# Two graph attentions in a GNN kernel: q and the exponentials in PSUM, weighted rows in buffers of their own, and the second attention in source order

## The chip, the cores and the metric

One core of one Trainium2 chip runs the whole program. The metric is the device time of one execution in microseconds (us). Engines: PE (TensorE), DVE (VectorE), ACT (ScalarE), POOL (GpSimd) and SP (SyncE); the last issues DMAs only. All data are float32.

## The reference

Four layers, each a graph step and a feed-forward step, on 3125 nodes of 256 features and 103125 edges (both directions and a loop at each node). The change touches the two attentions (layers 1 and 2). Layer 2's, cut down:

```
Q = (h @ Wq).reshape(n, H, HD); K, V likewise          # H = 8 heads
score = einsum('ehd,ehd->eh', Q[dst], K[src]) / sqrt(HD)
score = score + relu(efeat @ W1 + b1) @ W2 + b2        # the edge scores
m = segment_max(score, dst); ex = exp(score - m[dst])
alpha = ex / segment_sum(ex, dst)[dst]
out = segment_sum(alpha[:, :, None] * V[src], dst) @ Wo + bo
```
Layer 1's is of the same kind with 4 heads, keys and values by edge type, and no edge scores.

## The kernel before

The nodes are sorted by their number of edges and cut into 25 tiles of 128 nodes, one node to a partition. Tile t has CAPS[t] slots for edges (67, 44, 42 ... 22; 859 in all). A tile of more than KMAX = 44 slots is cut into parts: the first into two, so there are 26 parts, counted here from 0. A part is worked in chunks of CH = 4 slots: 225 chunks in all.

`attend` (L2299) does both attentions. For a part: q, the tile's 128 query rows, is loaded by SP (L2313). For every slot of a chunk POOL issues one indirect DMA (L2321) that gathers 128 rows of 2 KB (key and value of each node's neighbour) from a table in HBM into `kv`, by a column of indices in SBUF. DVE multiplies the key halves by q in place (L2326) and reduces the products to scores `s` (L2330). After the last chunk DVE adds the mask or edge scores (L2337), takes the maximum (L2339, L2341) and subtracts it (L2342); ACT takes exponentials (L2345); DVE sums them to `den` (L2347), and multiplies the value halves of each chunk by them in place (L2351). PE adds the weighted rows up by products with the identity into `u` in PSUM (L2361), two slots to a matmul. ACT copies one half of u to `agg` (L2366), DVE adds the other (L2367) and divides by den (L2389). `post` turns agg by PE (`turned_tile`, L2394, its copy L2400), multiplies it by the output weights and adds it to x (L833 in the first attention, L2650 in the second).

Buffers: `kv` has 13 of 8 KB per partition, and one comes free when PE has read its weighted rows. PSUM has two `u`.

The first attention carries a generator, `scores` (`edge_scores`, L1930): before each chunk's q product `next(beside, None)` emits a step of the second layer's edge scores: matmuls into `ph` and `psc`, relus by ACT (L1972), a turn by PE into `pst` (L1989). So its PE has work of its own.

The order of each engine's instructions is set by the framework's scheduler from its estimates, not by the source, except inside a block under `tc.manual_schedule(engines=...)`, where the engines named follow the source.

Of the kernel before, what the change touches and what calls it, by code (L numbers as in the profile page):

```python
# [23 lines left out]
F = mybir.dt.float32  # L24
I32 = mybir.dt.int32
U32 = mybir.dt.uint32
AF = mybir.ActivationFunctionType
OP = mybir.AluOpType
# [5 lines left out]
P = 128  # L34
# [32 lines left out]
class Net:  # L67
# [1862 lines left out]
    def edge_scores(self, ctx):  # L1930

        nc, tc, a, heads = self.nc, self.tc, self.a, 8
        pool = ctx.enter_context(tc.tile_pool(name="sc", bufs=1))
        wp = ctx.enter_context(tc.tile_pool(name="sc_w", bufs=2))
        ps_h = ctx.enter_context(tc.tile_pool(name="sc_h", bufs=1, space=PSUM))
        ps_s = ctx.enter_context(tc.tile_pool(name="sc_s", bufs=1, space=PSUM))
        w1 = pool.tile([P, D], F, name="w1")
        for s in range(2):  # L1940
            nc.sync.dma_start(w1[s * 64 : (s + 1) * 64], a["L2_gnn_W1"])
        b1 = self.columns(pool, a["L2_gnn_b1"], "b1")
        w2 = pool.tile([P, 2, 32], F, name="w2")
        nc.vector.memset(w2, 0.0)
        nc.sync.dma_start(w2[:, :, :heads], a["L2_gnn_W2"].rearrange("(c p) m -> p c m", p=P))
        b2 = pool.tile([P, 1], F, name="b2")
        nc.vector.memset(b2, 0.0)
        for k in range(4):
            nc.sync.dma_start(b2[32 * k : 32 * k + heads], a["L2_gnn_b2"].unsqueeze(1))

        def steps():
            for e0 in range(0, EP, STEP):
                pairs = min(STEP, EP - e0) // 1024
                runs = 2 * pairs
                ef = wp.tile([P, 2, 512], F, name="ef")
                for k in range(runs):
                    s, i = k % 2, k // 2
                    nc.sync.dma_start(
                        ef[s * 64 : (s + 1) * 64, i, :],
                        a["edge_t"][:, e0 + k * 512 : e0 + (k + 1) * 512],  # L1960
                    )
                hs = []
                for i in range(pairs):
                    h = wp.tile([P, 2, 2, 512], F, name="eh")
                    for f in range(2):
                        ps = ps_h.tile([P, 2, 512], F, name="ph")
                        for s in range(2):
                            half = slice(s * 64, (s + 1) * 64)
                            self.mm(
                                ps[:, s, :], [(w1[half, f * P : (f + 1) * P], ef[half, i, :])]  # L1970
                            )
                        nc.scalar.activation(h[:, f], ps, AF.Relu, bias=b1[:, f, :])  # L1972
                    hs.append(h)
                    yield
                ps = ps_s.tile([P, 512], F, name="psc")
                rows = 32 * runs
                for f in range(2):
                    for k in range(runs):
                        nc.tensor.matmul(
                            ps[32 * k : 32 * (k + 1)], w2[:, f, :], hs[k // 2][:, f, k % 2, :],  # L1980
                            start=f == 0, stop=f == 1,
                        )
                sc = wp.tile([P, 512], F, name="sc")
                nc.scalar.activation(sc[:rows], ps[:rows], AF.Identity, bias=b2[:rows])
                yield

                ps = ps_s.tile([P, 4, P], F, name="pst")
                for c in range(4):
                    nc.tensor.transpose(  # L1989
                        ps[:, c, :rows], sc[:rows].rearrange("h (p c) -> h c p", c=4)[:, c, :],  # L1990
                        self.ident[:rows, :rows],
                    )
                by_edge = wp.tile([P, 4, 4, heads], F, name="by_edge")
                nc.scalar.copy(
                    by_edge[:, :runs].rearrange("p k c h -> p c k h"),
                    ps[:, :, :rows].rearrange("p c (k r) -> p c k r", r=32)[:, :, :, :heads],
                )
                nc.scalar.dma_start(
                    self.score_d[e0 : e0 + runs * 512].rearrange(
                        "(k p c) h -> p k (c h)", c=4, p=P  # L2000
                    ),
                    by_edge[:, :runs].rearrange("p k c h -> p k (c h)"),
                )
                yield

        return steps()
# [292 lines left out]
    def attend(self, heads, q_d, table, rows, extra, post, beside=iter(())):  # L2299
# [3 lines left out]
        nc, tc = self.nc, self.tc  # L2303
        hd = D // heads
        with ExitStack() as sub:
            kvp = sub.enter_context(tc.tile_pool(name="at_kv", bufs=13))
            wp = sub.enter_context(tc.tile_pool(name="at_w", bufs=2))
            psu = sub.enter_context(tc.tile_pool(name="at_u", bufs=2, space=PSUM))
            held = None
            for t, k0, k, first, final in self.parts():  # L2310
                if first:
                    q = wp.tile([P, D], F, name="q")
                    nc.sync.dma_start(q, q_d[t * P : (t + 1) * P])  # L2313
                s = wp.tile([P, heads, KMAX], F, name="s")
                chunks = []
                for c0 in range(0, k, CH):
                    n = min(CH, k - c0)
                    kv = kvp.tile([P, CH, 2 * D], F, name="kv")
                    for c in range(n):
                        at = OFFS[t] + k0 + c0 + c  # L2320
                        nc.gpsimd.indirect_dma_start(  # L2321
                            out=kv[:, c, :], out_offset=None, in_=table,
                            in_offset=bass.IndirectOffsetOnAxis(ap=rows[:, at : at + 1], axis=0),
                        )
                    next(beside, None)
                    nc.vector.tensor_tensor(  # L2326
                        kv[:, :n, :D], kv[:, :n, :D], q.unsqueeze(1).to_broadcast([P, n, D]),
                        op=OP.mult,
                    )
                    nc.vector.tensor_reduce(  # L2330
                        s[:, :, c0 : c0 + n].rearrange("p h c -> p c h"),
                        kv[:, :n, :D].rearrange("p c (h d) -> p c h d", h=heads),
                        axis=AX.X, op=OP.add,
                    )
                    chunks.append((c0, n, kv))
# [6 lines left out]
                nc.vector.tensor_tensor(  # L2342
                    sk, sk, most.unsqueeze(2).to_broadcast([P, heads, k]), op=OP.subtract
                )
                nc.scalar.activation(sk, sk, AF.Exp)  # L2345
                den = wp.tile([P, heads], F, name="den")
                nc.vector.tensor_reduce(den, sk, axis=AX.X, op=OP.add)  # L2347
                u = psu.tile([P, 2, D], F, name="u")
                for c0, n, kv in chunks:
                    v = kv[:, :n, D:].rearrange("p c (h d) -> p c h d", h=heads)  # L2350
                    nc.vector.tensor_tensor(  # L2351
                        v, v,
                        s[:, :, c0 : c0 + n].rearrange("p h c -> p c h").unsqueeze(3).to_broadcast(
                            [P, n, heads, hd]
                        ),
                        op=OP.mult,
                    )
                    if n % 2:
                        nc.vector.memset(kv[:, n, D:], 0.0)
                    for c in range(0, n, 2):  # L2360
                        nc.tensor.matmul(  # L2361
                            u, self.ident, kv[:, c : c + 2, D:],
                            start=c0 == 0 and c == 0, stop=c0 + c + 2 >= k,
                        )
                agg = wp.tile([P, D], F, name="agg")
# [25 lines left out]
                )  # L2391
                post(t, agg)

    def turned_tile(self, psum, wp, rows):  # L2394

        ps = psum.tile([P, 2, P], F, name="tt")
        for c in range(2):
            self.nc.tensor.transpose(ps[:, c, :], rows[:, c * P : (c + 1) * P], self.ident)  # L2398
        sb = wp.tile([P, 2, P], F, name="tt_sb")
        self.nc.scalar.copy(sb, ps)  # L2400
        return sb
# [183 lines left out]
    def gnn2_ordered(self):  # L2585
        nc, tc, a = self.nc, self.tc, self.a
        heads, hd = 8, 32
        with ExitStack() as ctx:
# [44 lines left out]
            with ExitStack() as sub:  # L2633
# [9 lines left out]

                def post(t, agg):
                    at = self.turned_tile(psum, wp, agg)
                    po = psum.tile([P, D], F, name="o")
                    self.mm(
                        po, [(self.ones, bo)] + [(at[:, c, :], wo[:, c, :]) for c in range(2)]
                    )
                    nc.vector.tensor_tensor(self.x[:, t, :], self.x[:, t, :], po, op=OP.add)  # L2650

                self.attend(heads, q_d, kv_tab, self.row_src, extra, post)

    def gnn3_ordered(self):

# [257 lines left out]
```

## Time and profile before

| | us |
|---|---|
| median of 3 runs | 7778.85 (7748.85 to 7783.94) |
| the profiled execution | 7774.44 |
| its span | 7772.7 |
| first attention, first gather to the last update of x | 2346 to 3776 |
| second attention, the same | 4467 to 5804 |

Over the span PE is busy 4789.8 us (62%), POOL 3566.9 (46%), DVE 3206.6 (41%), ACT 1289.0 (17%); the mean granted clock of PE is 0.787. These shares average stages with different limits; the two attentions are read by their own stretches. In a row of grouped instructions the figures behind the bar are the busy time in us, the mean ns of one, and the engine's idle time just before them with what ended it. In a timeline row they are the start and length in us, the engine, line and operation, the tiles written and read, and in brackets the idle time before it.

### The profile page before, as it was taken

The page shows a single profiled execution, that of the slowest core. Times are in us where ns is not written, and L with a number is a line of the kernel's source. Part 1 is how long each engine was busy: PE and PEld are TensorE (multiplying, and loading weights), DVE is VectorE, ACT ScalarE, POOL GpSimd, SP SyncE. Part 2 cuts the span into 40 slices and gives each one's busy share as a digit, 9 for nine tenths or more (in the row PEclk, how much of TensorE's full clock was granted, in tenths as well). Part 3 has the DMA queues.
Part 4 walks back from the last instruction along what each step waited for, and adds up shares of the span by engine and source line. Part 5 has one row for each costly group of instructions (what it writes and reads, how often), then busy time and mean ns, then how long its engine had stood idle before and what let it go on. Part 6 is the DMA issues. An engine that isn't in the chain of part 4 may idle for free. (4 is left out here: it accounts for less than half of the span.)

```text
span 7772.7 us, 53026 instructions
## 1 busy us (share of the span) xinstructions
PE 4789.8 (62%) x17097; PEld 2917.2 (38%) x17097; DVE 3206.6 (41%) x5563; ACT 1289.0 (17%) x1898; POOL 3566.9 (46%) x4051
## 2 busy tenths in 40 slices
PE   1463313379885778878539423434452995498998
PEld 0352212244441222222338211111122995387554
DVE  7461101034224566666601255666672002496111
ACT  0000000022111222222013100000000221264222
POOL 3878787710006677776322377777752112100001
PEclk9786656689896888988669766666665997698999
DMA  6203542350336566666225255556641443221000
GB/s 246 86 18 123 178 178 69 92 163 9 139 138 185 166 188 199 198 186 175 86 99 181 90 166 170 171 172 178 183 137 72 168 170 107 102 73 38 9 13 22
DMA packets 424876, 999.32 MB, mean 129 GB/s; under 512 B 115151, under 2 KB 219057, under 8 KB 412942
## 3 DMA queue, kind: packets, MB, share of 16 engines
q0 software_dynamic: 206208, 656.36, 27.6%
q1 hardware_dynamic: 164616, 260.15, 10.3%
q10 hardware_dynamic: 53766, 79.32, 2.8%
q8 instruction: 141, 2.31, 0.1%
q14 instruction: 145, 1.19, 0.1%
HBM read 764.22 MB, written 231.45 MB: 128 GB/s over the span
## 5 line engine op out<-in xcount | busy, mean ns | idle before, releaser
L2321 POOL DMA_INDIRECT kv<-o_kv,row_et x859 | 974.9, 1135 | 432.9 <-issue 227.7
L2361 PE MATMUL u<-kv,ident 128*128 128x512 f32 x1740 | 880.9, 652 | 443.9 <-issue 332.7
L2321 POOL DMA_INDIRECT kv<-o_kv,row_src x859 | 1001.3, 1166 | 310.2 <-issue 229.3
L2145 POOL DMA_INDIRECT dense<-pair,place x859 | 907.5, 1056 | 294.5 <-issue 172.7
L2326 DVE TENSOR_TENSOR kv<-kv,q 128x1024 f32<-128x1024 f32 (+2 forms) x450 | 528.5, 1177 | 1022.1 <-DMA kv<-o_kv,row_src 561.6
L258 PE MATMUL g_u<-h_own,dense_rows 128*128 128x256 f32 x1250 | 389.2, 477 | 749.7 <-issue 234.9
L2361 PEld LDWEIGHTS u<-kv,ident 128*128 128x128 f32 x1740 | 340.7, 207 | 967.1 <-issue 792.0
L258 PEld LDWEIGHTS g_u<-h_own,dense_rows 128*128 128x128 f32 x1250 | 297.5, 246 | 841.1 <-issue 445.4
L2330 DVE TENSOR_REDUCE s<-kv 128x16 f32<-128x1024 f32 (+4 forms) x450 | 518.3, 1165 | 4.2
L2020 POOL DMA_INDIRECT out_dram<-x,order_i x25 | 24.6, 983 | 1051.5 <-DVE x L833 1006.6
L2351 DVE TENSOR_TENSOR kv<-kv,s 128x1024 f32<-128x1024 f32 (+2 forms) x450 | 496.5, 1169 | 0.0
L258 PE MATMUL c_hp<-c_xt,c_w 128*128 128x256 f32 x1536 | 389.6, 410 | 1.3 <-DVE c_xt L1251 1.3
L2028 POOL DMA_INDIRECT o_kv<-kv_rows,order_i x50 | 48.8, 976 | 716.9 <-ACT kv_rows L2524 483.9
L258 PE MATMUL ph<-ef,w 64*128 64x512 f32 x808 | 322.8, 709 | 88.6 <-issue 50.8
L258 PEld LDWEIGHTS c_hp<-c_xt,c_w 128*128 128x128 f32 x1536 | 371.7, 333 | 14.9 <-DVE c_xt L1251 7.5
L258 PE MATMUL c_o<-c_w,c_h 128*128 128x256 f32 x1536 | 351.9, 379 | 0.0
L2271 DVE TENSOR_TENSOR o_acc<-o_acc,g_u 128x256 f32<-128x256 f32 x125 | 52.3, 420 | 692.2 <-PE g_u L258 314.5
L1972 ACT ACTIVATE eh<-ph,b 128x1024 f32<-128x1024 f32 x202 | 224.9, 1114 | 499.5 <-PE ph L258 340.3
L2763 PE MATMUL u<-hs_all,eT_sb 128*128 128x256 f32 x1250 | 293.7, 382 | 21.9 <-ACT eT_sb L2759 21.9
L258 PEld LDWEIGHTS c_o<-c_w,c_h 128*128 128x128 f32 x1536 | 288.8, 191 | 34.9
L2398 PE MATMUL tt<-ident,agg 128*128 128x128 f32 x100 | 31.3, 412 | 420.8 <-DVE agg L2389 318.6
L833 DVE SCALAR_TENSOR_TENSOR x<-o,router_l,x 128x256 f32<-128x256 f32 x200 | 94.3, 484 | 459.2 <-PE o L258 459.2
(428 smaller groups left out, 7403.9 us busy)
## 6 DMA issues: line engine op xcount, KB each, us to landing
dense_rows<-dense SPq DMA_DIRECT2D x125, 640.0 KB
dense<-zero ACTq DMA_DIRECT2D x20, 3200.0 KB
ef<-in_edge_t_dram SPq DMA_DIRECT2D x202, 128.0 KB
number_d<-number SPq DMA_DIRECT2D x125, 160.0 KB
number<-number_d SPq DMA_DIRECT2D x25, 800.0 KB
c_x<-slot_d SPq DMA_DIRECT2D x64, 256.0 KB
result_d<-c_y SPq DMA_DIRECT2D x64, 256.0 KB
dense<-zero SPq DMA_DIRECT2D x5, 3200.0 KB
```

The source lines that it names most:

```text
L258: self.nc.tensor.matmul(ps, lhsT, rhs, start=i == 0, stop=i == len(pairs) - 1)
L833: self.nc.vector.scalar_tensor_tensor(self.x[:, t, :], y, w, self.x[:, t, :], op0=OP.mult, op1=OP.add)
L1972: nc.scalar.activation(h[:, f], ps, AF.Relu, bias=b1[:, f, :])
L2028: self.nc.gpsimd.indirect_dma_start(out=table, out_offset=bass.IndirectOffsetOnAxis(ap=self.order_i[:, t : t + 1], axis=0), in_=rows, in_o ...
L2145: nc.gpsimd.indirect_dma_start(out=dense[t], out_offset=bass.IndirectOffsetOnAxis(ap=place[:, at : at + 1], axis=0), in_=pair[:, at, :], i ...
L2271: nc.vector.tensor_tensor(acc[:, b, :], acc[:, b, :], ps, op=OP.add)
L2321: nc.gpsimd.indirect_dma_start(out=kv[:, c, :], out_offset=None, in_=table, in_offset=bass.IndirectOffsetOnAxis(ap=rows[:, at : at + 1], a ...
L2326: nc.vector.tensor_tensor(kv[:, :n, :D], kv[:, :n, :D], q.unsqueeze(1).to_broadcast([P, n, D]), op=OP.mult,)
L2330: nc.vector.tensor_reduce(s[:, :, c0 : c0 + n].rearrange("p h c -> p c h"), kv[:, :n, :D].rearrange("p c (h d) -> p c h d", h=heads), axis ...
L2351: nc.vector.tensor_tensor(v, v, s[:, :, c0 : c0 + n].rearrange("p h c -> p c h").unsqueeze(3).to_broadcast([P, n, heads, hd]), op=OP.mult,)
L2361: nc.tensor.matmul(u, self.ident, kv[:, c : c + 2, D:], start=c0 == 0 and c == 0, stop=c0 + c + 2 >= k,)
L2763: nc.tensor.matmul(u, et[:, j * P : (j + 1) * P], hs_all[:, b, :D], start=b == 0, stop=b == NT - 1,)
```

## The change

In both attentions, q is copied by ACT from its SBUF tile into a PSUM tile `q_ps`, from which DVE's product reads it; the exponentials are written to a PSUM tile `e`, from which den and the weighting products read; and the weighted value rows go into buffers of their own, `wv`, which PE's sums read. The first attention has 11 kv, 6 wv and one u; the second 12, 7 and two. To fit in PSUM, `psc` and `pst` share one buffer, and so do `turned_tile` and the output product `o`.

The second attention moves to a new function, `attend_in_order`, whose POOL, DVE, PE and ACT follow the source. There the weighting of a part is cut into steps: behind the scoring of each chunk of the next part come two chunks of it (three in parts of over 36 slots). Its sums by PE are emitted one chunk later (`sum_up`), and what follows them (`finish`, with `post`) is a list of steps, one to a chunk (`step_behind`), with empty steps between. q of the next tile is loaded at the second chunk of a tile's last part.

```
-            kvp = sub.enter_context(tc.tile_pool(name="at_kv", bufs=13))
+            kvp = sub.enter_context(tc.tile_pool(name="at_kv", bufs=11))
+            vp = sub.enter_context(tc.tile_pool(name="at_v", bufs=6))
-            psu = sub.enter_context(tc.tile_pool(name="at_u", bufs=2, space=PSUM))
+            psu = sub.enter_context(tc.tile_pool(name="at_u", bufs=1, space=PSUM))
...
                     nc.sync.dma_start(q, q_d[t * P : (t + 1) * P])
+                    q_ps = psu.tile([P, D], F, name="q_ps", bufs=2)
+                    nc.scalar.copy(q_ps, q)
...
-                        kv[:, :n, :D], kv[:, :n, :D], q.unsqueeze(1).to_broadcast([P, n, D]),
+                        kv[:, :n, :D], kv[:, :n, :D],
+                        q_ps.unsqueeze(1).to_broadcast([P, n, D]), op=OP.mult,
...
-                nc.scalar.activation(sk, sk, AF.Exp)
+                e = psu.tile([P, 512], F, name="e")[:, : heads * k]
+                e = e.rearrange("p (h c) -> p h c", h=heads)
+                nc.scalar.activation(e, sk, AF.Exp)
-                nc.vector.tensor_reduce(den, sk, axis=AX.X, op=OP.add)
+                nc.vector.tensor_reduce(den, e, axis=AX.X, op=OP.add)
...
+                    wv = vp.tile([P, CH, D], F, name="wv")
                     nc.vector.tensor_tensor(
-                        v, v,
-                        s[:, :, c0 : c0 + n].rearrange("p h c -> p c h").unsqueeze(3).to_broadcast(
+                        wv[:, :n, :].rearrange("p c (h d) -> p c h d", h=heads), v,
+                        e[:, :, c0 : c0 + n].rearrange("p h c -> p c h").unsqueeze(3).to_broadcast(
...
-                            u, self.ident, kv[:, c : c + 2, D:],
+                            u, self.ident, wv[:, c : c + 2, :],
```
The new function, without what is as in `attend`:

```
+    def attend_in_order(self, heads, q_d, table, rows, extra, post):
...
+            kvp = sub.enter_context(tc.tile_pool(name="at_kv", bufs=12))
+            vp = sub.enter_context(tc.tile_pool(name="at_v", bufs=7))
...
+                tc.manual_schedule(engines={E.Pool, E.DVE, E.PE, E.Activation})
...
+            def finish(part, u, most, den):
...
+                yield
+                agg = wp.tile([P, D], F, name="agg", bufs=3)
+                nc.scalar.copy(agg, u[:, 0, :])
+                yield
+                yield
+                nc.vector.tensor_tensor(agg, agg, u[:, 1, :], op=OP.add)
...
+                yield
+                yield from post(t, agg)
...
+            def weighed(part, chunks, e, most):
...
+                while len(unread) > 1:
+                    sum_up()
+                    step_behind()
+                unread.append(part)
+                den = wp.tile([P, heads], F, name="den", bufs=3)
+                nc.vector.tensor_reduce(den, e, axis=AX.X, op=OP.add)
+                u = psu.tile([P, 2, D], F, name="u", bufs=2)
+                for c0, n, kv in chunks:
...
+                    sums.append(lambda c=(c0, n, wv): add_up([c], u, k))
+                    yield
+                behind.append(finish(part, u, most, den))
...
+            for part in self.parts():
...
+                pace = 2 if k <= 9 * CH else 3
+                for c0 in range(0, k, CH):
...
+                    step_behind()
+                    sum_up()
+                    if c0 == CH and final:
+                        load_q(t + 1)
...
+                    step_weigh(pace)
+                    chunks.append((c0, n, kv))
+                while weigh:
+                    step_weigh(1)
```
And in what both call, and in the second attention's `post`:

```
-                ps = ps_s.tile([P, 4, P], F, name="pst")
+                ps = ps_s.tile([P, 512], F, name="psc").rearrange("p (c n) -> p c n", c=4)
...
-        ps = psum.tile([P, 2, P], F, name="tt")
+        ps = psum.tile([P, 2, D], F, name="o").rearrange("p a d -> p (a d)")
+        ps = ps[:, :D].rearrange("p (c n) -> p c n", c=2)
...
                     at = self.turned_tile(psum, wp, agg)
-                    po = psum.tile([P, D], F, name="o")
+                    yield
+                    po = psum.tile([P, 2, D], F, name="o")[:, 0, :]
...
+                    yield
+                    yield
+                    yield
                     nc.vector.tensor_tensor(self.x[:, t, :], self.x[:, t, :], po, op=OP.add)
 
-                self.attend(heads, q_d, kv_tab, self.row_src, extra, post)
+                self.attend_in_order(heads, q_d, kv_tab, self.row_src, extra, post)
```

## The prediction

> **What bounds the kernel now.** I read first the page (one core, span 7772.7 us), then its costliest groups: the three dearest contain the two gathers of L2321, one set per attention. Next the table by stretches for the two attentions, the waits of POOL, and the timeline at one part boundary.
>
> ```profile
> L2321 POOL DMA_INDIRECT kv<-o_kv,row_et x859 | 974.9, 1135 | 432.9 <-issue 227.7 <-PE u L2361 145.4 <-DVE kv L2351 14.6
> L2321 POOL DMA_INDIRECT kv<-o_kv,row_src x859 | 1001.3, 1166 | 310.2 <-issue 229.3 <-PE u L2361 55.6 <-DMA kv<-o_kv,row_src 12.5
> ```
> ```profile
> core 0: us, PE busy (x) PEld busy (x) DVE busy (x) ACT busy (x) POOL busy (x), PEclk, DMA share, GB/s
> 2346.00:3780.00 1434.00, 1088.52 (x2940) 350.42 (x2940) 864.47 (x1076) 300.68 (x385) 976.96 (x862) 0.84 0.63 180
> 4467.00:5804.00 1337.00, 530.35 (x1066) 231.72 (x1066) 831.98 (x953) 30.36 (x79) 1001.28 (x859) 0.66 0.59 171
> 3100.00:3300.00 200.00, 170.61 (x500) 53.89 (x500) 133.32 (x162) 54.15 (x69) 143.42 (x129) 0.93 0.68 197
> 4949.00:4966.00 17.00, 0.92 (x1) 0.50 (x2) 10.84 (x15) 0.46 (x1) 11.71 (x13) 0.50 0.74 215
> ```
> The attentions take 1434 and 1337 us. POOL is busy 75% of the second and DVE 62%; in the first PE has 76%, and 85% in its densest 200 us. The last row is a stretch in which every gather starts 1.25 us after the one before: DMA carries 215 GB/s there with 26% to spare, and elsewhere less, so it isn't the limit. Now how one gather behaves:
>
> ```profile
> 4962.17 0.95 POOL L2321 DMA_INDIRECT kv<-o_kv,row_src  x1 [0.30 <-issue]
> 4963.42 0.95 POOL L2321 DMA_INDIRECT kv<-o_kv,row_src  x1 [0.30 <-issue]
> 4964.90 9.50 DVE L2351 TENSOR_TENSOR kv<-kv,s 128x1024 f32<-128x1024 f32 x9
> 4969.11 6.12 POOL L2321 DMA_INDIRECT kv<-o_kv,row_src  x1 [4.74 <-PE u L2361]
> 4975.54 0.95 POOL L2321 DMA_INDIRECT kv<-o_kv,row_src  x1 [0.30 <-issue]
> ```
> The reader sees three things. An undisturbed gather takes 0.95 us and the next starts 0.30 us later: a pitch of 1.25 us. A gather may wait for a kv buffer that PE has still to read (4.74 us). And one that starts under the chain of products of L2351 is held until the chain is over: 6.12 us.
>
> I sorted all 859 gathers of the second attention by what DVE ran 0.2 us into each, and added up their time over 0.945 us: 220 under the q product L2326 are 90.0 us over, 89 under L2351 94.5 us over; but 153 under the reduction L2330 only 0.4, 293 under an idle DVE 0.2. All together 190; in the first attention 163. The two stretching forms read two operands from SBUF, the reduction one. What of two operands with one in PSUM?
>
> ```profile
> L2367 DVE TENSOR_TENSOR agg<-agg,u 128x256 f32<-128x256 f32 x26 | 10.7, 410 | 11.0 <-ACT agg L2366 7.3 <-issue 3.8
> L2389 DVE TENSOR_TENSOR agg<-agg,den 128x256 f32<-128x256 f32 x25 | 10.5, 421 | 0.1
> ```
> Nineteen gathers started under L2367 (u is in PSUM): 0.003 us over in all; 14 under L2650: 0.02; 31 under L833 in the first attention: 0.005; 12 under L2389 (both in SBUF): 0.7. And L2367 takes 410 ns against 421. So PSUM costs DVE nothing and frees POOL.
>
> **A rule against it.** The Trainium skill, "SBUF — State Buffer", section "Who interferes with whom", says that a DVE instruction with two SBUF inputs contends with GpSimd instructions that read SBUF, not with those that only write, and it infers that descriptor generation needs only the write side, so that tensor_tensor had not stalled DMA in its probe. By that inference products would not delay gathers and this part of the sum would be 0 instead of 353. The rows above speak against the inference (these gathers do read their index column from SBUF); I take the trace.
>
> **The change, part by part: second attention (before: first gather 4467.1, last ends 5776.0, result 5803).**
> - Floor: 859 gathers x 1.25 = 1074 us, against 1309 now. Of the 235 between, 190 are stretching and 48 are waits beyond the 0.305 us gap (310.2 - 859 x 0.305).
> - q and e in PSUM: -190, save for L2337, L2342 and L2389, which keep two SBUF inputs (4 us of the 190): -186.
> - kv buffers come free after DVE's product instead of after PE's sum, but there are 12 in place of 13. With nine chunks to a part POOL can run 3 chunks (15 us) ahead. The first buffer is free 12 us after the part's end: last chunk lands (gather to DVE 3.8 us), product and reduction 2.4, the part's four small operations 2.5, the next first chunk's product and reduction 2.4, den and one product 1.6. So no wait; with ten chunks (4 parts) POOL is 10 us ahead and waits 2, with eleven (2 parts) 5 us ahead and waits 7. Sum 22 us in place of 48: -26.
> - Order by chunks: DVE does two or three of the old part's products behind each chunk, so the chain of 10 us goes. Per chunk: four operations of about 1.15 us of busy time, against 5.0 us of gathers. DVE's 832 us in 1137 is 73%: covered by POOL. If that cover failed, each DVE us counts.
> - Steps spaced over chunks: the agg copy, the sum, turned_tile, po and the x update each come a chunk (5 us) behind what they wait for, so DVE, PE and ACT, now in source order, do not stand in front of a late wait. If one step stood, the next chunk's product would queue behind it on DVE: 26 parts x about 1 us; I take 10 us.
> - q: SP issues the load (25 x 0.32 us; it has nothing else here) nearly a tile earlier, and ACT adds 25 copies of about 0.37 us (row L2400) beside its 30 us of work: hidden. POOL's order of gathers stays. An ACT write to PSUM has no row; nearest is the L2366 copy out of it, 372 ns.
> - wv: same number of products, memsets and matmuls. Tail after the last gather: 27 us now, the same after.
> Sum: -186 - 26 + 10 = -202; bounds -235 (floor) and -100 (DVE stands behind ordered waits half the time gained). I take -200.
>
> A second rule bears on q_ps. "PSUM — Partial Sum Buffer", section on bank collisions, has every pair of engines on one 2 KiB bank kept apart by a dependency. Two 1 KB q_ps buffers in one bank would make ACT's write of the next q stand between DVE's products of this one, and behind the q load (estimate: as long as a gather's 3.8 us, and the copy): 25 x 4.2 = 105 us of DVE time per attention, most of it inside DVE's 27% idle. No run here shows it; I take 0, as the bank count (8 in the first attention before, if every tile fills whole ones) fits separate banks.
>
> **First attention (1434 us).**
> - Stretching -163. Waits beyond the gaps are 171 us (145 for PE's sums). In part 13 (of 0 to 25) PE ends its sums 44 us after DVE's last product (3207.2 to 3251.5), nearly a part late, as edge-score matmuls fill PE. Now kv does not wait for them; wv (6 buffers) does, and DVE behind it.
> - With POOL at its floor this stage would be 1074 + 36 us of ends = 1110. But PE has 1088 us of work. Above 85%, its densest stretch, nothing shows it can go: 1088.5 / 0.853 = 1276.
> - One u buffer, psc and pst sharing one, tt and o sharing one: each user comes after the other's reader anyway (the sums of a part follow the copy of the last); PE loses perhaps 26 x 0.4 us, inside its 15%. Eleven kv: parts of eleven chunks get no lead, 2 x 12 us, also inside. 25 copies on an ACT that is 21% busy: 0.
> I take 1434 - 1276 = -158; bounds 0 (order of PE stays what it is and sets the pace) and -324.
>
> **Sum.** -200 - 158 = -358. The profiled execution took 7774.4 (span 7772.7 and 1.7 around it): 7416. The median of the runs is 4.4 above it: about **7421 us**.
>
> **The rivals.**
> - PE sets the first attention already: no gain there, the second as above: 7779 - 200 = 7579. For: PE at 85%, edge scores in the same queue. Against: PE waited while POOL was stretched. 0.17.
> - The first goes nearly free (1150, PE's clock above 0.93): 7779 - 209 - 284 = 7286. Against: 1088 us of PE work. 0.08.
> - Slower: DVE stands before its seventh to ninth product, because wv has six buffers and PE, with a single u, sums each part 44 us late; scores, then gathers, queue behind DVE. By part 13 a third of 44 us and the wait for u: 20 us; unabsorbed in 26 parts 520: 7941. It decides from 358/26 = 14 us per part. Against: kv frees six buffers at once, 30 us of gathers. 0.11.
> - The change doesn't do what it says: operands in PSUM do not free POOL. Then only buffer waits go, -26 and some -60: 7690; and if products from PSUM were slower too, no change. Against: L2367, L2650, L833. 0.04, of which 0.03 within 0.5%.
>
> **How the numbers follow.** The likeliest case (0.60) gives 7421, its own range 7320 to 7520. From 7290 to 7650 leaves out the slow case, the PSUM failure and half of the free one: 0.19. About 0.5% (39 us) is what a measurement here can tell from no change. Faster: 0.60 + 0.17 + 0.08 + 0.01 = 0.86; same: 0.03; slower: 0.11.
>
> **What would show it.** Gathers' mean near 950 ns in both sets, with no 6 us ones; second attention near 1137 us, DVE's waits there for DMA and not for PE or ACT; the products' mean still near 1220 ns; PE near 85% in the first. I am wrong if gathers stay above 1100 ns, if DVE waits for PE before the products into wv for more than 5 us a part, or if the first attention keeps 1400 us with POOL idle.

## The result and the profile after

The changed kernel took 7886.77 us (median of 4 runs, 7841.36 to 7912.81) against 7763.91 for the kernel before beside it (4 runs): a ratio of 1.014, 95% interval 1.0101 to 1.0179. It is slower, by about 1.4%; 7421 had been forecast. The profiled execution took 7869.77, span 7868.0. On a chip met later the same kernel is faster than before by 3.4%, so most of what follows asks what the first chip does that that one does not.

First the costliest groups of instructions, the gathers of the two attentions (busy time, mean ns of one, idle time of POOL before them and what ended it):

```profile
L2327 POOL DMA_INDIRECT kv<-o_kv,row_et x859 | 813.1, 947 | 677.4 <-DVE wv L2360 350.2 <-issue 234.4 <-DVE wv L2368 17.3
L2534 POOL DMA_INDIRECT kv<-o_kv,row_src x859 | 812.3, 946 | 506.8 <-DVE wv L2504 248.1 <-issue 242.9 <-DMA kv<-o_kv,row_src 14.0
```

The stretching is gone: 947 and 946 ns a gather instead of 1135 and 1166. But POOL's idle time rose by 245 us in the first attention (432.9 to 677.4) and by 197 in the second (310.2 to 506.8), and what ends most of it is a product into `wv`, which sets a kv buffer free. The table by stretches, from the first gather to the end of the last copy out of `u` (columns as in the prediction: us, then PE, PEld, DVE, ACT, POOL busy):

```profile
2333.00:3842.00 1509.00, 1074.31 (x2930) 347.33 (x2930) 851.76 (x1043) 306.81 (x406) 812.78 (x859) 0.83 0.59 171
4537.00:5890.00 1353.00, 538.25 (x1058) 225.88 (x1058) 848.26 (x945) 34.63 (x102) 812.19 (x859) 0.67 0.58 169
```

Before, cut in the same way (this cut is used for every kernel below):

```profile
2347.00:3765.00 1418.00, 1081.51 (x2930) 348.17 (x2930) 852.55 (x1022) 299.02 (x383) 974.40 (x859) 0.85 0.63 182
4467.00:5800.00 1333.00, 528.51 (x1060) 230.84 (x1060) 830.56 (x949) 29.99 (x78) 1001.28 (x859) 0.66 0.59 171
```

No engine is near its limit: POOL lost 162 and 189 us of work, and the stages became 91 and 20 us longer. The waits say who is late (engine and line, waited for: us in all, times, longest):

```profile
ACT agg L2448 <- remote: 870.1, 18, 62.8
...
POOL kv L2327 <- DVE wv L2360: 350.2, 59, 29.2
...
POOL kv L2534 <- DVE wv L2504: 248.1, 19, 23.1
DVE o_acc L2271 <- remote: 248.0, 21, 22.1
...
DVE agg L2451 <- ACT agg L2448: 138.2, 10, 23.7
...
DVE wv L2504 <- remote: 54.7, 7, 11.7
```

`remote` means that no instruction of this core with a recorded end fits the moment at which the wait ended. ACT's copy out of `u` (L2448) can only wait for PE; DVE's add to `agg` (L2451) waits for that copy, 138.2 us in all, where the same add in before (L2367) waited 7.3 us in the second attention. One part of the second attention, the records of PE, DVE, ACT and POOL from the timeline (start, us, engine, line, shape and count, idle before):

```profile
5025.65 9.97 PE L2437 MATMUL u<-wv,ident 128*128 128x512 f32 x16 [3.52 <-DVE wv L2504]
...
5067.31 2.07 PE L2437 MATMUL u<-wv,ident 128*128 128x512 f32 x2 [6.19 <-DVE wv L2512]
```
```profile
5044.86 1.22 DVE L2504 TENSOR_TENSOR wv<-kv,e 128x1024 f32<-128x1024 f32 x1 [1.98 <-remote]
5056.07 1.22 DVE L2504 TENSOR_TENSOR wv<-kv,e 128x1024 f32<-128x1024 f32 x1 [7.59 <-remote]
5066.56 0.42 DVE L2504 TENSOR_TENSOR wv<-kv,e 128x256 f32<-128x256 f32 x1 [9.28 <-remote]
...
5084.68 0.42 DVE L2451 TENSOR_TENSOR agg<-agg,u 128x256 f32<-128x256 f32 x1 [6.04 <-ACT agg L2448]
```
```profile
5084.27 0.37 ACT L2448 COPY agg<-u 128x256 f32<-128x256 f32 x1 [61.81 <-remote]
5084.54 0.42 ACT L2566 ACTIVATE e<-s 128x288 f32<-128x288 f32 x1
```
```profile
5074.60 0.95 POOL L2534 DMA_INDIRECT kv<-o_kv,row_src  x1 [0.30 <-issue]
5090.02 0.94 POOL L2534 DMA_INDIRECT kv<-o_kv,row_src  x1 [14.48 <-DVE wv L2504]
```

The first row holds 16 matmul records, the sums of the first four chunks (four records to a chunk), recorded as over by 5035.6. Yet DVE's eighth, ninth and tenth products, which reuse the `wv` buffers of chunks one to three, start only at 5044.9, 5056.1 and 5066.6: one chunk's completion about every 11 us. The last sum is recorded as over at 5069.4; ACT copies at 5084.27, 14.9 us later. By then POOL had stopped for want of kv buffers (last gather at 5074.60). What stands behind the late copy in source order is late with it: ACT's exponentials of the next part (5084.54), DVE's add (5084.68), and behind both the product that sets the next kv buffer free, for which POOL's gather at 5090.02 had waited 14.48 us. I call the time from the last recorded sum of a part to ACT's copy the lag, counted from the end of ACT's preceding instruction where that comes later. Added up over the parts of the second attention it is 425 us after, 12 before; in the first 45 and 15. PE has no recorded work in the 425 us, and DVE is busy in 30% of them; in the two waits of 7.59 and 9.28 us above DVE did nothing, while the gathers went on every 1.25 us.

That a recorded end need not be the true one is what the Trainium skill says, "Perfetto Trace Analysis", section "Per-instruction lifecycle": a TensorE record starts when the operands are fetched, its end is computed, and the semaphore is pushed later, when PSUM has acknowledged the writes. The rows agree: the matmul rows look prompt, and only those who wait for PE show 15 us. They do not show whether PE itself was late or only its signal.

### The profile page after: what moved, and what is told of

Read it like the earlier page. It is cut to its first block, busy times and chain, and to the rows that moved or that the text cites. A ratio compares the mean times of both kernels' runs of the same rounds, so it can differ in the third digit from the quotient of the medians.

```text
span 7868.0 us, 52190 instructions
## 1 busy us (share of the span) xinstructions
PE 4787.3 (61%) x17097; PEld 2909.0 (37%) x17097; DVE 3220.3 (41%) x5563; ACT 1302.5 (17%) x1948; POOL 3216.8 (41%) x4051
## 5 line engine op out<-in xcount | busy, mean ns | idle before, releaser
L2327 POOL DMA_INDIRECT kv<-o_kv,row_et x859 | 813.1, 947 | 677.4 <-DVE wv L2360 350.2
L2534 POOL DMA_INDIRECT kv<-o_kv,row_src x859 | 812.3, 946 | 506.8 <-DVE wv L2504 248.1
L2437 PE MATMUL u<-wv,ident 128*128 128x512 f32 x870 | 466.1, 692 | 329.9 <-DVE wv L2504 221.9
L2370 PE MATMUL u<-wv,ident 128*128 128x512 f32 x870 | 462.4, 659 | 79.7 <-DVE agg L2376 63.6
L2437 PEld LDWEIGHTS u<-wv,ident 128*128 128x128 f32 x870 | 186.9, 223 | 594.3 <-issue 450.5
L2332 DVE TENSOR_TENSOR kv<-kv,q_ps 128x1024 f32<-128x1024 f32 (+2 forms) x225 | 261.5, 1168 | 299.6 <-DMA kv<-o_kv,row_et 238.3
L2542 DVE TENSOR_TENSOR kv<-kv,q_ps 128x1024 f32<-128x1024 f32 (+2 forms) x225 | 261.8, 1164 | 201.7 <-DMA kv<-o_kv,row_src 195.7
L2360 DVE TENSOR_TENSOR wv<-kv,e 128x1024 f32<-128x1024 f32 (+2 forms) x225 | 258.1, 1165 | 165.1 <-PE u L2370 82.5
L2271 DVE TENSOR_TENSOR o_acc<-o_acc,g_u 128x256 f32<-128x256 f32 x125 | 52.3, 420 | 665.6 <-PE g_u L258 332.4
L2580 PE MATMUL o<-ident,agg 128*128 128x128 f32 x100 | 29.1, 389 | 458.9 <-DVE agg L2474 259.2
```

What stands on the lines that cost most here:

```text
L2327: nc.gpsimd.indirect_dma_start(out=kv[:, c, :], out_offset=None, in_=table, in_offset=bass.IndirectOffsetOnAxis(ap=rows[:, at : at + 1], a ...
L2332: nc.vector.tensor_tensor(kv[:, :n, :D], kv[:, :n, :D], q_ps.unsqueeze(1).to_broadcast([P, n, D]), op=OP.mult,)
L2360: nc.vector.tensor_tensor(wv[:, :n, :].rearrange("p c (h d) -> p c h d", h=heads), v, e[:, :, c0 : c0 + n].rearrange("p h c -> p c h").uns ...
L2370: nc.tensor.matmul(u, self.ident, wv[:, c : c + 2, :], start=c0 == 0 and c == 0, stop=c0 + c + 2 >= k,)
L2437: nc.tensor.matmul(u, self.ident, wv[:, c : c + 2, :], start=c0 == 0 and c == 0, stop=c0 + c + 2 >= k,)
L2534: nc.gpsimd.indirect_dma_start(out=kv[:, c, :], out_offset=None, in_=table, in_offset=bass.IndirectOffsetOnAxis(ap=rows[:, at : at + 1], a ...
```

## The experiments

Theories at the start. A: the gathers, now at their full pitch of 1.25 us without pauses, hold PE's completions back. B: the small `wv` ring and the order are at fault. C: PE runs at a low clock between its small bursts, and so ends late. D came with the first results: the late completions belong to some chips only.

**Four kernels on another chip.**

The kernel before, with `q` and `e` in PSUM alone:

```
-  q.unsqueeze(1) ...            +  q_ps.unsqueeze(1) ...
-  nc.scalar.activation(sk, sk, AF.Exp)
+  nc.scalar.activation(e, sk, AF.Exp)      # e in PSUM; v = v * e in place
```


> The kernel before with q and e in PSUM in both attentions and nothing else new: 13 kv buffers, products in place, the planner's order, two u (first attention: one q_ps, psc shared, o shared). Theory A (the gathers' full pitch holds PE's sums back: what was gained by not stretching gathers comes back as late sums): the gathers' mean falls to about 950 ns in both sets, but kv buffers, which wait for PE here, come free late, and the second attention stays within 40 us of 1337, the whole within 1% of before. Theory B (the order by chunks and the small wv ring are at fault, the operands in PSUM are good by themselves): second attention near 1150 us (1337 less 186), the first between 1280 and 1400, the whole 7450 to 7560.

Measured: 7296.47 us, ratio 0.962 (0.9603 to 0.9637) to 7577.95 for before; stages 1234 and 1173, lag 1 us or less in all. Theory B's numbers, and better. But before took 7578 here, not 7764: this was another chip.

Extra matmuls behind each chunk's sums; in the first attention, `pst` in its own bank:

```
+  for _ in range(8):
+      nc.tensor.matmul(warm, self.ident, self.ident, start=True, stop=True)
...
-  ps = ps_s.tile([P, 512], F, name="psc")...    +  ps = ps_s.tile([P, 4, P], F, name="pst")
-  name="q_ps", bufs=2                           +  name="q_ps", bufs=1
```


> After, with eight extra 128x128 matmuls of the identity behind each chunk's sums in the second attention (their result is not used), and with pst in a bank of its own and one q_ps in the first. Second attention, theory C (PE falls to a low clock between its small bursts, and the sums end late for that): the sums' ends come within 2 us of the record, the second attention falls from 1360 to 1150 to 1220 us. Theory A (held back by the gathers): the lag of 10 to 39 us from the last recorded sum to the agg copy stays, 1350 us or more. First attention: if the shared psc bank costs what PE waits for it more than before (128 us against 65), it falls from 1528 to about 1465; if not, it stays within 15 us.

Measured: 7305.96, ratio 0.964 (0.962 to 0.9659); stages 1303 and 1118, no lag.

A memset behind each gather; in the first attention, two `u`:

```
+  nc.gpsimd.memset(idle, 0.0)            # idle: 64 columns
...
-  u = psu.tile([P, 2, D], F, name="u")   +  ... name="u", bufs=2)
-  name="q_ps", bufs=2                    +  name="q_ps", bufs=1
```


> After, with a 64-column GpSimd memset behind each gather of the second attention, and with two u and one q_ps in the first. Second attention, theory A: with a pause in each pitch the sums' lag goes to near 0 and POOL's waits for wv with it; the time is then set by the pitch, 859 x (1.25 + the memset's 0.1 to 0.2), 1160 to 1250 us. Theory C (PE's low clock): lag and waits stay, 1360 us or more. First attention: if the single u is at fault (PE waits 64 us there for the agg add), 1528 falls to about 1465; if not, it stays within 15 us.

Measured: 7343.56, ratio 0.9689 (0.967 to 0.9709); stages 1305 and 1152, no lag. The memset takes 0.17 us but widens the pitch by only 0.03, to 1.28.

Second attention in order, products in one chain; first attention of before:

```
-  pace = 2 if k <= 9 * CH else 3         +  pace = len(range(0, KMAX, CH))
+  sum_up()                               # behind every product
```


> First attention of before; second attention of after, but with all products of a part in one chain behind the next part's first chunk, each chunk's sum placed behind its product. First attention 1434 within 15 us. Second: theory C (small bursts leave PE slow): the sums follow the chain as before, lag near 0, 1150 to 1220 us. Theory A: gathers flow during the chain, the lag stays 10 us or more in most parts, 1320 us or more.

Measured: 7350.78, ratio 0.9699 (0.9679 to 0.9718); stages 1342 and 1117, no lag.

None of these four shows the lag, neither the three whose edits were meant to act in different ways nor the one that keeps the planner's order. That fits D better than A or C, and only the unchanged kernel could tell.

**A third chip.** After, unchanged:

> After, unchanged. Theory D (PE's late completions belong to the chip that the first comparison ran on, not to the kernel: on the chip of the four runs so far none shows them, although pacing, warming and chaining were meant to act in different ways): the lag from the last recorded sum to the agg copy is 0 in both attentions, the first near 1304 us, the second near 1118, the whole near 7305 against 7578 for before, a ratio near 0.964. Theories A and C (the kernel's own pattern makes the completions late, and each of the three edits cured it): the lag of 10 to 39 us is back, the second attention is near 1350 and the whole above 7500.

Measured: 7318.33, ratio 0.9663 (0.9647 to 0.9679) to 7572.63. Its stretches, waits, and one part's end:

```profile
2225.00:3532.00 1307.00, 1054.07 (x2930) 344.75 (x2930) 851.33 (x1042) 306.75 (x406) 814.62 (x859) 0.88 0.68 198
4215.00:5338.00 1123.00, 522.70 (x1058) 220.60 (x1058) 857.60 (x945) 35.27 (x102) 816.21 (x859) 0.71 0.69 203
```
```profile
ACT agg L2448 <- PE u L2437: 503.3, 21, 32.2
...
POOL kv L2327 <- DVE wv L2360: 179.8, 63, 9.6
...
POOL kv L2534 <- DVE wv L2504: 21.9, 7, 7.0
```
```profile
4696.59 1.98 PE L2437 MATMUL u<-wv,ident 128*128 128x512 f32 x4 [1.42 <-DVE wv L2504]
```
```profile
4698.61 0.37 ACT L2448 COPY agg<-u 128x256 f32<-128x256 f32 x1 [23.55 <-PE u L2437]
```

The same instructions, and ACT starts 0.04 us after the last recorded sum (4696.59 + 1.98 = 4698.57). `remote` has gone from these rows, POOL's wait for `wv` in the second attention falls from 248.1 to 21.9 us, and the stage from 1353 to 1123. D holds, and the four runs before have told nothing of A or C, since there was no lag to take away. Before, unchanged, for its profile:

> Before, unchanged, for a profile from the chip of these runs. Theory D: first attention near 1342 us (as in the run that kept it), second within 30 us of 1333; the gathers' mean 1150 to 1170 ns in both. If before's second attention is over 100 us shorter here than in the first profile, a comparison of stages across the two chips says nothing.

Measured: 7563.28 (one execution); stages 1349 and 1335, no lag. Before's second attention is the same on both kinds of chip (1333 and 1335); its first is 69 us shorter here, and its first gather starts at 2221 instead of 2347 us.

First attention in place as in the first of these experiments, second as in after:

```
   first attention:  q, e in PSUM; kv bufs=13; products in place; u bufs=2; q_ps bufs=1
   second attention: attend_in_order, unchanged
```


> The cheaper half of each kind: first attention with q and e in PSUM, products in place and 13 kv buffers (1234 us in the first of these runs, against 1304 with six wv), second attention as in after. If the stages add up: 7296 less the 55 us that the second attention in order is shorter than in place (1173 against 1118), about 7241. If the first attention's gain in place came from the planner's order around it, it stays at 7296.

Measured: 7254.33, ratio 0.9568 (0.9551 to 0.9585); stages 1244 and 1122. The stages add up, and it is the fastest version on this kind of chip, 64 us ahead of after.

**A chip of the first kind** (before at 7771.65). After, unchanged:

> After, unchanged, beside before. On a chip with prompt completions: 0.966 of before, second attention 1122 us, lag 0. On one like that of the first comparison: 1.01 of before, second attention about 1350, lag 10 to 39 us. Which of the two it is on the third chip shows how common each is.

Measured: 7869.07, ratio 1.0113 (1.0045 to 1.0182); stages 1518 and 1355, lag 44 and 396, and part by part nearly the first profile's: 36, 7, 31, 32, 17 us for the first five against 36, 8, 32, 32, 19. The behaviour is repeatable. The in-place kernel again:

> The kernel with the first attention in place and the second in order, unchanged, for a further chip: 0.957 of before where PE's completions come at once (7254 us on the last chip); on a chip like that of the first comparison its second attention has the lag of 10 to 39 us (1350 us), and the whole is within 2% of before.

Measured: 7883.77, ratio 1.0139 (1.0073 to 1.0206); stages 1552 and 1329, lag 47 and 450. The best version of one kind of chip loses on the other.

Fewer kv buffers in the first attention, products in place in the second:

```
-  name="at_kv", bufs=13                  +  name="at_kv", bufs=11       # first attention
-  wv[:, :n, :]..., v, e...               +  v, v, e...                  # second, kv bufs=13
```


> The last kernel (first attention in place, second in order) with two edits: 11 kv buffers in place of 13 in the first attention, and in the second the products written in place (no wv, 13 kv). First attention: if the fewer kv buffers are why the changed kernel's first attention takes 1307 us against 1244 in place, it goes to about 1300; if the ring of six wv is (DVE cannot be more than six products ahead of PE), it stays within 20 us of 1244. Second: if buffers of their own for weighted rows carry the gain over the 1173 us of the planner's order in place, it goes to about 1170; if the hand-written order carries it, it stays near 1122. On a chip whose PE completions come late, in place is the worse of the two in both.

Measured: 7829.26, ratio 1.0071 (1.0044 to 1.0099); stages 1546 and 1247, lag 16 and 303. Against 1552 the two buffers cost nothing in the first. In the second, in place is better here by 82 us (1247 against 1329), the opposite of what I expected. There kv waits for PE's sum itself, and POOL stops for PE's sums or for `remote` 40 times, 142 us in all, against 17 stops of 224 us for DVE's products into `wv`. That the shorter, more frequent stops let the completions through (the lag is 303 against 450) is my reading; no run tests it.

Memsets behind all gathers:

```
+  nc.gpsimd.memset(idle, 0.0)            # 64 columns in the first attention, 512 in the second
```


> After with a GpSimd memset behind every gather, 64 columns in the first attention (pitch 1.28 us as measured in the paced run), 512 in the second (an estimate from the 64 columns' 0.17 us: up to 0.8 us more, a pitch of 1.9 us, 1630 us). On a chip with prompt completions this only costs: first attention 1307 plus about 20, second 1630. On a chip like the first: if it is the dense flow of gathers that holds PE's completions back, the second attention's lag of 10 to 39 us goes to near 0 at the wide pitch; if it is the chip at any pitch, it stays.

Measured: 7961.77 (one execution); stages 1502 and 1468, lag 54 and 0. The first attention tells nothing, since its memsets ran in an earlier stage and its pitch stayed at 1.25. In the second the pitch was 1.65, and the lag is gone in every part:

```profile
ACT agg L2450 <- PE u L2439: 647.2, 21, 37.0
```

ACT's longest waits for `u` are again matched to recorded ends, with no `remote`. So on a chip of this kind it is the dense flow of gathers that holds the completions back, as A says. C falls: the granted clock is 0.67 in this stage, as in after's, with the lag gone. That left two questions: from which pitch, and whether the first attention is under the same rule.

**Three paced kernels, on both kinds.** First attention of before, second in order at a pitch of 1.39:

```
+  nc.gpsimd.memset(idle, 0.0)            # 192 columns, second attention
```


> First attention of before; second of after with a 192-column GpSimd memset behind each gather (estimate from 0.17 us for 64 columns and 0.54 us for 512: 0.28 us, a pitch of 1.38). Theory A (dense gathers hold PE's completions back on some chips): on a chip like that of the first comparison the lag shrinks below 10 us in most parts, the second attention takes 859 x 1.38 = 1185 plus 25, about 1210, against 1333 of before and 1353 of after, and the whole is about 1.5% faster than before. On a chip with prompt completions the same 1210, and with the first attention as before about 0.984. If the lag stays at 1.38, 1300 or more on the former kind.

> First attention of before, second in order at a pitch of 1.38. On a chip with late completions (before near 7770 us): if 1.38 is wide enough, lag near 0 and a second attention near 1246 us as on the other kind, 1333 for before, so the whole about 0.989 of before; if not, lag of 5 us or more in half of the parts and 1290 us or more. On a chip with prompt completions (before near 7570): 7489 us again.

Measured: 7489.49, ratio 0.9884 (0.9859 to 0.9909) with prompt completions, and 7704.31, ratio 0.9896 (0.9861 to 0.9931) with late ones; second attention 1246 and 1259. On the latter chip a lag of 194 us is left, in 14 of the 26 parts, but the stage is only 13 us longer; DVE's add waits for ACT's copy 6.7 us in all there.

In place in both, memsets ahead of the first attention's gathers and behind the second's:

```
+  nc.gpsimd.memset(kv[:, c, :64], 0.0)   # first attention, kernel in place
+  nc.gpsimd.memset(idle, 0.0)            # 64 columns, second, products in place
```


> First attention with q and e in PSUM, products in place, 13 kv, and a 64-column GpSimd memset into each kv column ahead of its gather (an estimate: 0.2 to 0.4 us more, a pitch of 1.45 to 1.65, a floor of 1250 to 1420); second in order, in place, 13 kv, 64 columns of memset behind each gather (pitch 1.28). Theory A on a chip like that of the first comparison: the first attention, 1552 us unpaced, falls to 1300 to 1440, since PE's edge-score and sum completions come on time; if it is the planner's order or the PSUM sharing that costs there, it stays above 1500. Second near 1240 as without memsets, if 1.28 is still too dense. With prompt completions: first 1280 to 1440, second about 1180.

> First attention in place with 64-column memsets ahead of the gathers, second in order, in place, at a pitch of 1.28. On a chip with late completions: first attention 1552 us unpaced; Theory A: below 1480, with few lags; if it is something else there, above 1500. Second 1247 within 25 us. With prompt completions: 7324 us again.

Measured: 7323.56, ratio 0.9667 (0.9643 to 0.9691), stages 1282 and 1148; and 7783.61, ratio 0.9995 (0.9965 to 1.0025), stages 1498 and 1259. The first attention's median pitch was only 1.26, far under my estimate, and 1498 falls between what the theories gave.

After, with wide pacing in both:

```
+  nc.gpsimd.memset(kv[:, c, :256], 0.0)  # first attention
+  nc.gpsimd.memset(idle, 0.0)            # 320 columns, second
```


> After with a 256-column memset into each kv column ahead of its gather in the first attention (an estimate: a pitch of 1.6 to 1.8, 1380 to 1550 us), and a 320-column memset behind each gather in the second (pitch 1.48, 1275 plus 25, 1300 us). On a chip like that of the first comparison: lag near 0 in the second, 1300 us; first attention at its pitch rather than at 1509. With prompt completions the same times.

> After with 256-column memsets ahead of the gathers in the first attention (1385 us on a prompt chip, median pitch 1.68) and a pitch of 1.50 in the second (1334 us). On a chip with late completions, Theory A: the same 1385 and 1334 within 30 us with lags near 0, where the unpaced stages took 1509 and 1353; if the first is held back by something else, 1450 or more. With prompt completions: 7610 us again.

Measured: 7610.35, ratio 1.0044 (1.0027 to 1.006), with prompt completions; 7742.01, ratio 0.9955 (0.9923 to 0.9987), with late ones. The stretches, first the prompt chip's, then the other's:

```profile
2231.00:3615.00 1384.00, 1088.20 (x2930) 353.07 (x2929) 857.93 (x1042) 307.00 (x406) 1064.31 (x1716) 0.85 0.66 187
4302.00:5636.00 1334.00, 546.98 (x1057) 226.97 (x1058) 868.40 (x945) 35.01 (x102) 1147.88 (x1718) 0.68 0.59 171
```
```profile
2328.00:3713.00 1385.00, 1088.64 (x2930) 353.72 (x2930) 858.34 (x1042) 306.88 (x406) 1065.71 (x1717) 0.85 0.66 187
4413.00:5748.00 1335.00, 545.46 (x1058) 226.40 (x1058) 866.18 (x945) 35.27 (x102) 1147.82 (x1718) 0.68 0.60 171
```

At this pitch (median 1.68 in the first attention, 1.50 in the second) both kinds of chip take the same time to within 1 us, with no lag on either. The first attention, 1509 and 1518 us unpaced, takes 1385: there too the flow of gathers holds PE back. Lag and length of the second attention on chips of the late kind, by pitch (all with `wv`):

| pitch, us | lag, us in all | second attention, us | the same on a prompt chip |
|---|---|---|---|
| 1.25 (after) | 425 and 396 | 1353 and 1355 | 1122 |
| 1.39 | 194 | 1259 | 1246 |
| 1.50 | 0 | 1334 | 1334 |
| 1.65 | 0 | 1468 | not tried |

What is open: what differs between the chips. The gathers themselves do not: from the start of a chunk's last gather to the product that waited for it, the median in after's second attention is 3.77 us on a late chip and 3.78 on a prompt one, and a gather takes 946 and 950 ns. A memset also spaces out what follows the gathers, DVE's products among it; that DVE stood idle in waits of 7.59 and 9.28 us speaks against those, but no run slowed DVE alone. Whether the bytes of the gathers or the issuing of them is what counts, whether PE or only its signal is late, and whether a chip is late by itself or by what else it was doing, was not tried.

## Why the prediction was wrong

**Stretching (-190 and -163): right.** 1001.3 to 812.3 us and 974.9 to 813.1, and much the same on every chip; the products with one operand in PSUM take 1163 to 1168 ns, against 1169 and 1177 before. The trace was to be trusted over the rule on interference.

**Second attention (-200): the size was right, on another chip.** With prompt completions POOL's busy time falls by 186 us and its idle time by 28: gathers 1312.0 to 1097.5 us, 214 shorter. On the first chip 189 us of busy time went and 197 of idle time came. The step that failed is "Steps spaced over chunks", put at 10 us: a chunk, 5 us, behind what they wait for, DVE, PE and ACT in source order were not to "stand in front of a late wait". DVE stood 138.2 us before its add to `agg` alone, and its idle time that no gather ended comes to 394 us in this stage, against 10 on the prompt chip. The step that let kv buffers come free after DVE's product, "so no wait", failed with it, at a smaller price. It took DVE's products as waiting for nothing but DVE, but they also wait for `wv`, and `wv` for PE's completion (61 us of the 394). Under both lies a term that the sum does not have: I took completions at the recorded ends. In before that had been so, to within 12 us. As I read it, that was because its gathers stood still under each chain of products (4.74 us of wait and a gather of 6.12 in the part shown with the prediction), just while PE summed, so that the stalls that the change removed were also the pauses in which PE's completions got through; no run tests this by itself. I had read DMA at 215 GB/s "with 26% to spare" as proof that a dense flow costs nothing.

**First attention (-158): mis-sized on any chip.** It came to -42 with prompt completions (1349 to 1307): 171 us of stretching went, and POOL's idle time grew by 127 us, to 479.7; products into `wv` end 179.8 us of that. In place it is 1244, with PE busy for 1062 us, 85%: that fits the limit that I took from the densest 200 us, and the wrong part was that six `wv`, 11 kv and one `u` would cost nothing. A second `u` (1305) or a bank for `pst` (1303) alone brings nothing, and two kv buffers brought nothing on a late chip; what remains is the ring of six with the planner's order around it, which was not tried by itself, so the cause stays open. The profile of after from the prompt chip points to the order: DVE stands only 20.4 us for want of a `wv` there and 410.6 us for gathers, while POOL waits for the products that stand behind these scorings in DVE's order. On the first chip, with late completions, it was +91.

**The rivals.** The slower one named the right chain (DVE before its later products, `wv` behind PE, gathers behind DVE), put it in the first attention only, and gave the cause as PE's work. Late completions, of which it says nothing, make most of the distance from the forecast (1.014 of before, against 0.966 without them; 0.954 was forecast), so that it had the direction is in part luck. It was given 0.11. That operands in PSUM do not free POOL fell at once. Of the signs named, the gathers' 950 ns came true; "DVE's waits there for DMA and not for PE or ACT" did not (195.7 us for DMA, 138.2 for ACT's copy), and "the first attention keeps 1400 us with POOL idle" was the warning that came true.

## What to carry to other kernels

Ask of a stall before removing it what gets done during it: here, as far as the paced runs tell, the pauses in the gathers were the windows in which another engine's results arrived. A TensorE end in the trace is no proof that its result was announced; read the start of whoever waits for it, and watch for `remote`. In source order everything behind a late wait is late too: a distance of one chunk, 5 us, does not cover lags of up to 39 us. And measure on more than one chip: the same edit was 3.4% faster on one kind and 1.1 to 1.4% slower on the other, while the version that was faster on both (one chip of each), by 1.0 to 1.2%, keeps the old first attention and spaces the second's gathers at 1.39 us.

## What the runs showed of the hardware

In three of the six sets of runs PE's completions came late by up to 39 us while gathers of 256 KB followed each other every 1.25 us, and at once when they came every 1.50 us (on one of these chips) or 1.65 us (on another); in the other three sets, on three chips, they were prompt. (The late sets are the first one, whose chip is not on record, and two more on a chip each.) It is not bound to this change: in the first profile of before, DVE waits 288.7 us for `remote` ahead of L2271, in an earlier stage, and in before's profile from a prompt chip that row is missing. The SBUF page of the Trainium skill ("SBUF — State Buffer", section "SBUF: two separate sides") has transfers and engines on separate ports, unable to slow each other; the pacing runs show a transfer stream that delays PE's announced results on some chips (a lag of 425 us at a pitch of 1.25, none at 1.50), though not by which path.

A GpSimd memset of 64 columns between two gathers is nearly free: 0.17 us of it widened the pitch by 0.03, since the gap ahead of the next gather shrank from 0.30 us to 0.16.
